# An attention block: the residual added by an accumulating transfer, more tiles for the first set, a later bias

## Chip, cores, metric

One core of one Trainium2 chip. The metric is the device time of one execution in microseconds (us), the median of several.

## The reference

Sixteen images of 512 channels x 1024 positions, in fp32: group norm, three projections, attention with four heads, an output projection, and the input added at the end.

```python
xn = ((xg - mu) * jax.lax.rsqrt(var + EPS)).reshape(b, c, h, w)
xn = xn * norm_gamma[:, None, None] + norm_beta[:, None, None]
qkv = jnp.einsum('oc,bchw->bohw', qkv_w, xn) + qkv_b[:, None, None]
...
attn = jax.nn.softmax(jnp.einsum('bhnd,bhmd->bhnm', q, k) * scale, axis=-1)
out = jnp.einsum('bhnm,bhmd->bhnd', attn, v)
...
out = jnp.einsum('oc,bchw->bohw', proj_w, out) + proj_b[:, None, None]
return x + out
```

## The kernel before

All products with weights are done by Strassen's scheme at two levels: seven outer products in four groups, seven inner products in each, so that TensorE multiplies less and VectorE adds more. While one head's attention runs (scores s, exponentials p, sums po), the other work is laid between its steps: under head 0 a q/k product, under head 1 the output projection of the image before and the norm of the next image, under head 2 the next q/k product, under head 3 the next v product. Line numbers in profiles shift a little between kernels; the names of the tiles do not.

The end of a projection, with its residual loaded ahead:

```python
        def prepare(which, r):                       # called some units ahead
            ...
            t = ys[which, r] = ypool.tile([P, HALF], F32, tag="y", ...)   # 4 buffers
            dma = nc.gpsimd.dma_start(t, x[b, ts(o, P), ts(half, HALF)])
            tc.add_manual_dep(dma.ins, last_eviction[b].ins.name, ...)

        def finish(which, r, a, c):
            ...
            nc.vector.scalar_tensor_tensor(t, a, projb_sb[:, o : o + 1], t, ALU.add, ALU.add)
            nc.vector.tensor_add(t, t, c)
            nc.gpsimd.dma_start(out[b, ts(o, P), ts(half, HALF)], t)
```

The norm's one instruction on GpSimd, and the last image's bias:

```python
        ve = gn.tile([P, k], F32, tag="ve", name="ve")
        self.last = nc.vector.tensor_scalar_add(ve, pv[:, :k], EPS)
        rstd = gn.tile([P, k], F32, tag="rstd", name="rstd")
        nc.gpsimd.tensor_tensor(rstd, ve, self.neghalf, ALU.pow)
        # cut: VectorE makes scale and shift of it, ScalarE then normalises the next image
    ...
    def last_bias():
        for c in range(NCC):
            nc.scalar.activation(late["y"][c], late["y"][c], AF.Identity, bias=projb_sb[:, c : c + 1])
```

## Time and profile before

| | before |
|---|---|
| time | 3199.4 us (five runs, 3198.9 to 3201.3) |
| span of the profiled run | 3198.0 us |
| TensorE, VectorE, ScalarE, GpSimd busy | 99, 82, 45, 17% |
| mean period of one image | 196.56 us |

The mean period is taken from GpSimd's timeline: the rstd instruction runs once per image, at 142.76 us for the second image and at 2894.55 for the last, so (2894.55 - 142.76) / 14. What lies ahead of the first of these is the start, what lies behind the last is the end.

### The profile page before, as it was taken

What the parts mean: (1) busy time and instruction counts of PE and PEld (TensorE: products, weight loads), DVE (VectorE), ACT (ScalarE), POOL (GpSimd) and SP (SyncE); (2) the same over time, 40 slices, a digit from 0 to 9 for tenths busy, and PEclk for the clock granted to TensorE, in tenths of its full rate; (3) what the DMA queues carried; (4) which work ended last, traced back from release to release, by engine and by line L of the source; (5) the groups of instructions that cost most, each with busy time, mean ns of one, the idle gap of its engine ahead of it and who ended that gap; (6) DMA issues with size and microseconds to landing.
All of it is one profiled execution on the core that took longest, in us unless ns stands there. A gap on an engine that the chain in (4) does not pass through costs nothing.

```text
span 3198.0 us, 34052 instructions
## 1 busy us (share of the span) xinstructions
PE 3161.4 (99%) x10474; PEld 2183.2 (68%) x10474; DVE 2633.2 (82%) x4625; ACT 1443.5 (45%) x2709; POOL 528.1 (17%) x922
## 2 busy tenths in 40 slices
PE   8999999999999999999999999999999999999999
PEld 6566676776766766677666676667676676766664
DVE  8878878788797888878788787987879978788784
ACT  2534435354353543535435454353534545344442
POOL 0011221112211112211122111222112221112100
PEclk9999999999999999999999999999999999999999
DMA  4565554545545455454554546555455564555531
GB/s 160 195 197 166 184 171 143 177 149 190 171 155 168 154 189 174 159 166 143 183 173 166 167 139 197 166 170 174 136 182 169 175 186 133 176 166 185 170 128 38
DMA packets 209387, 526.92 MB, mean 165 GB/s; under 512 B 32816, under 2 KB 65840, under 8 KB 209200
## 3 DMA queue, kind: packets, MB, share of 16 engines
q1 hardware_dynamic: 128992, 276.88, 28.5%
q0 software_dynamic: 66240, 212.39, 19.7%
q10 hardware_dynamic: 13968, 35.41, 3.5%
q8 instruction: 86, 1.41, 0.2%
q14 instruction: 101, 0.83, 0.1%
HBM read 389.56 MB, written 135.00 MB: 164 GB/s over the span
## 4 chain that ended last, share of the span: by engine, by line
PE 85%; DVE 6%; issue 3%; DMA 3%; ACT 2%; POOL 1%; SPq 0%; POOLq 0%; DVEq 0%
PE po L874 24%; PE s L778 23%; PE qk_x L553 12%; PE qk_y L553 8%; PE v_x L553 6%; PE v_y L553 4%; PE pp_x L553 4%; PE pp_y L553 3%; ACT x L85 1%; DMA y<-in_x 1%; DVE pp_r L620 1%; POOL rstd L67 1%; DVE pp_r L573 1%; DVE tot L792 1%; DVE o L884 1%
## 5 line engine op out<-in xcount | busy, mean ns | idle before, releaser
L874 PE MATMUL po<-p,v 128*128 128x512 f32 x2048 | 1049.2, 594 | 0.5 <-ACT o L881 0.5
L778 PE MATMUL s<-qk,qk 128*128 128x512 f32 x2048 | 1047.9, 593 | 1.3 <-ACT p L784 1.3
L784 ACT ACTIVATE p<-s 128x512 f32<-128x512 f32 x1024 | 610.8, 597 | 942.4 <-PE s L778 898.4
L874 PEld LDWEIGHTS po<-p,v 128*128 128x128 f32 x2048 | 602.9, 303 | 317.5 <-issue 211.4
L792 DVE TENSOR_TENSOR tot<-tot,p 128x1024 f32<-128x1024 f32 x385 | 469.0, 1218 | 160.0 <-ACT p L784 159.8
L778 PEld LDWEIGHTS s<-qk,qk 128*128 128x128 f32 x2048 | 387.6, 190 | 89.7 <-issue 28.5
L553 PEld LDWEIGHTS qk_x<-qk_t,w 128*128 128x128 f32 x1344 | 250.7, 190 | 176.9 <-issue 76.7
L553 PE MATMUL qk_x<-qk_t,w 128*128 128x256 f32 x1344 | 358.5, 383 | 4.5 <-ACT qk_u L453 3.0
L453 ACT COPY qk_u<-qk_x 128x512 f32<-128x512 f32 (+1 forms) x256 | 136.3, 532 | 232.0 <-PE qk_x L553 230.0
L717 POOL DMA_DIRECT2D vd<-vu x120 | 66.7, 557 | 906.9 <-DVE vu L709 903.0
L573 DVE TENSOR_TENSOR qk_r<-qk_y,qk_u 128x512 f32<-128x512 f32 (+1 forms) x256 | 158.0, 617 | 40.6 <-ACT qk_u L453 26.3
L553 PE MATMUL pp_x<-pp_t,w_proj 128*128 128x256 f32 x630 | 169.4, 385 | 5.9 <-ACT pp_u L453 5.7
L762 POOL DMA_DIRECT2D out_y<-y x120 | 66.2, 552 | 619.2 <-DVE y L761 589.0
L722 POOL DMA_DIRECT2D v<-vd x240 | 140.6, 593 | 164.3 <-DMA vd<-vu 58.7
L573 DVE TENSOR_TENSOR v_r<-v_y,v_u 128x512 f32<-128x512 f32 (+1 forms) x120 | 76.3, 636 | 110.6 <-ACT v_u L453 80.3
L553 PE MATMUL v_x<-v_t,w_v 128*128 128x256 f32 x630 | 166.6, 381 | 0.0
L527 POOL DMA_DIRECT2D kept_t<-qk_t x240 | 129.3, 541 | 225.9 <-DVE qk_t L523 158.4
L553 PEld LDWEIGHTS pp_x<-pp_t,w_proj 128*128 128x128 f32 x630 | 115.5, 190 | 73.0 <-issue 22.2
L553 PEld LDWEIGHTS v_x<-v_t,w_v 128*128 128x128 f32 x630 | 118.4, 190 | 55.3 <-issue 19.1
L553 PE MATMUL qk_y<-x,w 128*128 128x256 f32 x512 | 142.2, 379 | 0.0
L652 DVE SCALAR_TENSOR_TENSOR qk<-qk_r,qkb_sb,qk_r 128x512 f32<-128x512 f32 x192 | 137.6, 743 | 1.6
L453 ACT COPY v_u<-v_x 128x512 f32<-128x512 f32 (+1 forms) x124 | 66.3, 535 | 160.4 <-PE v_x L553 130.3
(204 smaller groups left out, 4483.2 us busy)
## 6 DMA issues: line engine op xcount, KB each, us to landing
kept_t<-qk_t POOLq DMA_DIRECT2D x180, 256.0 KB, 2.9
w<-kept SPq DMA_DIRECT2D x90, 512.0 KB, 4.1
v_t<-kept_t SPq DMA_DIRECT2D x180, 256.0 KB, 2.9
w<-kept SPq DMA_DIRECT2D x90, 384.0 KB, 3.5
rinv<-row ACTq DMA_DIRECT2D x63, 512.0 KB, 4.8
x<-in_x POOLq DMA_DIRECT2D x60, 512.0 KB, 4.4
vd<-vu POOLq DMA_DIRECT2D x120, 256.0 KB, 3.0
v<-vd POOLq DMA_DIRECT2D x240, 128.0 KB, 4.2
```

The costliest lines, as they stand in the source:

```text
L453: nc.scalar.copy(t[n][:, :width], t["x"][:, :width])
L527: nc.gpsimd.dma_start(t, to)
L553: nc.tensor.matmul(acc[:, ts(i, Q)], have["w"][t][:, i, slot, :], inner(i, bn), start=(first and i == 0), stop=True, skip_group_check=True,)
L573: nc.vector.tensor_add(dst, view(a), view(c))
L652: nc.vector.scalar_tensor_tensor(st[b, h][:, ts(half, HALF)], a, qkb_sb[:, i : i + 1], c, ALU.add, ALU.add)
L717: nc.gpsimd.dma_start(rows[which][ts(h, P), :], u)
L722: nc.gpsimd.dma_start(vs[b, pair][ts(q, BLK), half].rearrange("m h (k i) j -> m (h k) (i j)", k=n), rows[which].rearrange("(k m) (q e) -> ...
L762: nc.gpsimd.dma_start(out[b, ts(o, P), ts(half, HALF)], t)
L778: nc.tensor.matmul(sc, ks[b, h][:, ts(j, P)], qs[b, h][:, ts(half, HALF)], start=True, stop=True)
L784: exps[s] = nc.scalar.activation(ps[s][:, ts(half, HALF)], sc, AF.Exp, scale=SCALE)
L792: added[b, h, j] = nc.vector.tensor_add(tot[b, h][:, i], tot[b, h][:, i], ps[s][:, i])
L874: nc.tensor.matmul(po[b, h][:, i], v_block(b, h, j), ps[s][:, i], start=(j == 0), stop=(j == NB - 1),)
```

## The change

The intent is to take work off VectorE and to close gaps at both ends:

1. The residual is no longer loaded into y and added by VectorE. VectorE adds the two halves of the product and the bias, and a transfer that adds brings x into the finished tile; then the tile is stored. A load and 120 additions go.
2. In the first set, groups 1 and 3 take their sums of inputs in p buffers (homes "C"), and the weights of group 2 two idle tiles.
3. The last image's bias is placed behind an exponential on ScalarE.

```diff
+        own = first and (site, g) == (0, 2)
         w = [
-            wpool.tile([P, 2, m, P], F32, tag=f"w{t}", ...)
+            (lpool if own else wpool).tile([P, 2, m, P], F32, tag=("tt", "rinv")[t] if own else f"w{t}", ...)
 ...
+            if homes[g] == "C":
+                if k % 2 == 0:
+                    pairs[g] = ppool.tile([P, N], F32, tag="p", name=f"{name}_{g}_{m}")
+                t = pairs[g][:, ts(k % 2, HALF)]
 ...
-            "ABBB" if pair else "ABAB" if b > 0 else "BBBB",
+            "ABBB" if pair else "ABAB" if b > 0 else "BCBC",
 ...            # prepare() and its calls go
         def finish(which, r, a, c):
             ...
+            t = ypool.tile([P, HALF], F32, tag="y", ...)
             nc.vector.scalar_tensor_tensor(
-                t, a, projb_sb[:, o : o + 1], t, ALU.add, ALU.add
+                t, a, projb_sb[:, o : o + 1], c, ALU.add, ALU.add
             )
-            nc.vector.tensor_add(t, t, c)
+            nc.gpsimd.dma_start(t, x[b, ts(o, P), ts(half, HALF)], accum_op=ALU.add)
             nc.gpsimd.dma_start(out[b, ts(o, P), ts(half, HALF)], t)
 ...
     def last_bias():
+        with tc.issue_after(exps[max(exps)].ins):
             for c in range(NCC): ...
```

More of the change, by code (lines that the diff above doesn't have):

```diff
@@ L359, in group_weights @@
         n = len(group)
+        own = first and (site, g) == (0, 2)
         w = [
-            wpool.tile([P, 2, m, P], F32, tag=f"w{t}", name=f"w{t}_{site}_{g}")
+            (lpool if own else wpool).tile(
+                [P, 2, m, P], F32, tag=("tt", "rinv")[t] if own else f"w{t}",
+                name=f"w{t}_{site}_{g}",
+            )
             for t, m in enumerate(PARTS)
@@ L487, in strassen, with two_levels @@
         return [units[i] for i in ORDER]
-    def two_levels(name, site, b, blocks, finish, sums="make", homes="BBBB", prepare=None):
+    def two_levels(name, site, b, blocks, finish, sums="make", homes="BBBB"):
         R = {}
-        haves = [{} for _ in OUTER]
+        haves, pairs = [{} for _ in OUTER], {}
         def part(g, i, row=None):
@@ L504, in sum_tile @@
             tag = f"in_{m}" if homes[g] == "B" else f"ot{2 + k // 2}{k % 2}"
-            t = tpool.tile([P, HALF], F32, tag=tag, name=f"{name}_{g}_{m}")
+            if homes[g] == "C":
+                if k % 2 == 0:
+                    pairs[g] = ppool.tile([P, N], F32, tag="p", name=f"{name}_{g}_{m}")
+                t = pairs[g][:, ts(k % 2, HALF)]
+            else:
+                t = tpool.tile([P, HALF], F32, tag=tag, name=f"{name}_{g}_{m}")
             haves[g][m] = t.rearrange("p (i q) -> p i q", q=Q)
@@ L597, in group_units @@
                 unit(lambda: inner_sum("t3"), p2), unit(lambda: inner_sum("t4"), p6),
-                unit(lambda: load("t2"), lambda: ready(g), p5), unit(lambda: load("t1"), p7),
+                unit(lambda: load("t2"), p5), unit(lambda: load("t1"), p7),
                 unit(lambda: load("t3"), p4), unit(lambda: load("t4"), p3, end),
@@ L608, in first_sums @@
                         make_sum(g, m)
-        results = {1: ("c11",), 2: ("c22", "c21"), 3: ("c12",)}
-        def ready(g):
-            for which in results.get(g, ()) if prepare else ():
-                for r in range(2):
-                    prepare(which, r)
         pending = []
@@ L735, in proj_groups, with finish @@
     def proj_groups(b):
-        ys = {}
-        def place(which, r):
-            return 2 * (int(which[1]) - 1) + r, int(which[2]) - 1
-        def prepare(which, r):
-            o, half = place(which, r)
-            t = ys[which, r] = ypool.tile([P, HALF], F32, tag="y", name=f"y_{b}_{o}_{half}")
-            dma = nc.gpsimd.dma_start(t, x[b, ts(o, P), ts(half, HALF)])
-            tc.add_manual_dep(
-                dma.ins, last_eviction[b].ins.name,
-                mybir.DependencyInfo(
-                    mybir.DependencyClass.Sync, mybir.DependencyReason.DATA
-                ),
-                reason="residual",
-            )
-        def finish(which, r, a, c):
-            o, half = place(which, r)
-            t = ys.pop((which, r))
-            nc.vector.scalar_tensor_tensor(
-                t, a, projb_sb[:, o : o + 1], t, ALU.add, ALU.add
-            )
-            nc.vector.tensor_add(t, t, c)
+        def finish(which, r, a, c):
+            half, o = int(which[2]) - 1, 2 * (int(which[1]) - 1) + r
+            t = ypool.tile([P, HALF], F32, tag="y", name=f"y_{b}_{o}_{half}")
+            nc.vector.scalar_tensor_tensor(
+                t, a, projb_sb[:, o : o + 1], c, ALU.add, ALU.add
+            )
+            nc.gpsimd.dma_start(t, x[b, ts(o, P), ts(half, HALF)], accum_op=ALU.add)
             nc.gpsimd.dma_start(out[b, ts(o, P), ts(half, HALF)], t)
-        return two_levels(f"pp_{b}", "proj", b, lambda: ob[b], finish, prepare=prepare)
+        return two_levels(f"pp_{b}", "proj", b, lambda: ob[b], finish)
     ps, tot, po, rinv, last_eviction = {}, {}, {}, {}, {}
@@ L941, in last_bias @@
     def last_bias():
-        for c in range(NCC):
-            nc.scalar.activation(
-                late["y"][c], late["y"][c], AF.Identity, bias=projb_sb[:, c : c + 1]
-            )
+        with tc.issue_after(exps[max(exps)].ins):
+            for c in range(NCC):
+                nc.scalar.activation(
+                    late["y"][c], late["y"][c], AF.Identity, bias=projb_sb[:, c : c + 1]
+                )
     fine = []
```

## The prediction

> **What bounds the kernel now.** I read the page's busy rows first, then TensorE's clock and its waits, then the stretches where TensorE was not busy.
>
> ```profile
> PE 3161.4 (99%) x10474; PEld 2183.2 (68%) x10474; DVE 2633.2 (82%) x4625; ACT 1443.5 (45%) x2709; POOL 528.1 (17%) x922
> PEclk9999999999999999999999999999999999999999
> ```
>
> TensorE is busy in 3161.4 of 3198.0 us at full clock, and VectorE has 3198.0 - 2633.2 = 565 us free. Whatever the change does on VectorE can count only where TensorE stands waiting: 36.6 us of recorded idle in all. The view of waits, TensorE alone, the first 90 us and then 90 to 3150 us:
>
> ```profile
> PE pm L52 <- DVE mean L50: 10.6, 1, 10.6
> PE qk_x L553 <- DVE qk_t L523: 1.2, 1, 1.2
> PE qk_x L553 <- DVE w L390: 1.1, 1, 1.1
> ...
> PE pp_x L553 <- ACT pp_u L453: 5.7, 14, 0.4
> PE qk_y L553 <- DVE qk_t L523: 3.8, 4, 2.0
> PE qk_x L553 <- ACT qk_u L453: 2.4, 2, 1.5
> ```
>
> The columns are the total in us, the number of waits and the longest. The 10.6 us is the start, before the statistics are there. In the whole middle, 3060 us, VectorE makes TensorE wait 3.8 us in four waits, and no wait there names the residual tile y. The stretches view shows the two other holes. Its columns are PE, PEld, DVE, ACT, POOL busy time, with counts.
>
> ```profile
> 32.00:36.00 4.00, 4.00 (x20) 3.54 (x19) 1.92 (x6) 0.59 (x1) 0.00 (x0) 1.00 0.92 325
> 36.00:40.00 4.00, 4.00 (x19) 3.36 (x19) 1.26 (x3) 1.17 (x2) 0.00 (x0) 1.00 0.24 72
> 40.00:44.00 4.00, 4.00 (x20) 3.53 (x19) 2.06 (x5) 0.93 (x2) 0.00 (x0) 1.00 0.25 66
> ...
> 56.00:60.00 4.00, 2.96 (x13) 1.79 (x11) 4.00 (x8) 1.50 (x3) 0.00 (x0) 1.00 0.25 84
> 60.00:64.00 4.00, 2.69 (x10) 1.74 (x10) 3.91 (x7) 0.64 (x2) 0.00 (x0) 1.00 0.11 33
> 64.00:68.00 4.00, 2.25 (x8) 1.28 (x9) 3.94 (x11) 0.57 (x2) 0.00 (x0) 1.00 0.32 113
> 68.00:72.00 4.00, 3.56 (x11) 1.83 (x11) 3.79 (x8) 1.14 (x3) 0.00 (x0) 1.00 0.22 63
> ```
>
> From 32 to 44 us VectorE has 12 - (1.92 + 1.26 + 2.06) = 6.8 us free while TensorE is full; from 56 to 72 us VectorE is full (15.6 of 16 us) and TensorE lacks 16 - (2.96 + 2.69 + 2.25 + 3.56) = 4.5 us. This is the first set: VectorE is the bound for some 16 us there, because it could not start earlier. The second hole is late, in the chain that ended last:
>
> ```profile
> 3007.51 5.78 DMA y<-in_x
> ...
> 3023.44 7.30 DMA y<-in_x
> ...
> 3056.59 5.56 DMA y<-in_x
> ```
>
> These loads are not the residuals of the projections but the last image's, which a ScalarE bias (line 943) takes up at once. The waits of this stretch have "ACT y L943 <- DMA y<-in_x: 9.6, 4, 2.8". ScalarE runs in order, so its copies out of PSUM stand behind. In the stretches of 5 us TensorE lacks 1.52 us (3010 to 3015), 0.84 (3030 to 3035) and 0.48 (3060 to 3065): 2.8 us.
>
> **What the Trainium skill says.** (1) "Perfetto Trace Analysis", section Per-engine timelines, Tensor Engine: matmul ends are estimated. The trace agrees: eight 128x256 matmuls in a row take 1.73 us in the chain, 0.216 us each, while their mean row says 379 to 385 ns. So I also count: one image has 4 x 98 matmuls of 128x256 and 256 of 128x512 (0.430 us each), 84.7 + 110.1 = 194.8 us of work, and its period is 1122.04 - 925.65 = 196.4 us (starts of the rstd instruction in the chain). Only 1.6 us per image is open to any change. (2) "VectorE: DVE Perf Modes": fp32 tensor_tensor takes (N+151)/0.96 ns, 691 ns for 512. The trace has 682 ns for line 761, about the same. (3) "DMA: Bandwidth & Descriptors", Rules for kernel authors: an accumulating DMA is issued from GpSimd, reads its destination and writes it later, and a dependent access has to wait for its semaphore. So the store of y must wait on GpSimd until the addition has landed. No accumulating transfer is in the trace before. (4) The same page, Anatomy of one DMA: 2.0 us + bytes / 436e3, so 2.6 us for 256 KB. The trace has 4.0 us for the residual's load and 2.9 for the store; I use those.
>
> **The change part by part.**
>
> *Residual.* Removed: 120 additions at line 761 x 682 ns = 81.8 us of VectorE, and 120 loads of 256 KB. Line 758 stays one scalar_tensor_tensor of the same shape, 120 x 745 ns, now adding the two products. Added: 120 accumulating transfers, issued at 0.54 us each like line 745, so GpSimd's issue time stays equal. VectorE falls to about 2551 us. Nearly all of that lies under TensorE's work: per image 81.8 / 15 = 5.5 us in a stretch of 50 us where VectorE has 16% free. At the end of each projection VectorE is dense, and the norm's small operations come between; finishing those 0.7 to 1.4 us sooner may start the normalisation sooner, but the wait seen there is on ScalarE's pp_u copy (0.4 us per image), behind normalisations on ScalarE that stay as long as they are. I give it -1 us over 15 images.
>
> *More tiles for the first set.* Groups 1 and 3 of the first product take their sums from the p buffers in place of the tiles that group 0 and 2 hold, and the weights of group 2 take two idle tiles. The release that ends the waits is a read by TensorE: the waits of the SP queue have
>
> ```profile
> SPq L375 <- PE qk_y L553: 32.2, 10, 9.8
> ```
>
> and the timeline has the sums for group 1 first at 42.54 us after an idle of VectorE. Eight sums at about 0.37 us back to back are 3.0 us, two s3 blocks and four weight sums at 0.41 us are 2.5 us: 5.5 us of VectorE work can move into the 6.8 us that are free. With VectorE that much earlier from 44 us on, the 4.5 us hole should shrink by the same, but not wholly: p has three buffers, four such pair tiles want them, and the finishes still come at TensorE's pace. I take 4.0 us of 4.5.
>
> *Last bias.* It is put behind an exponential that is already issued, so the loads have landed when ScalarE comes to it. Saved: the 2.8 us. Cost: four 128x1024 activations of 1.15 us now stand among exponentials that are spaced 1.72 us apart at 0.60 us each; a score tile can come about 0.1 us late each time. I take 2.5 us net.
>
> Sum: -1.0 - 4.0 - 2.5 = -7.5 us on 3200.6, that is 3193.
>
> **The rivals.**
>
> *The store waits on GpSimd, and VectorE behind it.* The y pool has 4 buffers. Before, a tile was free one store (2.9 us) after its last addition; now it goes through the addition (about 4.0 us, estimated from the load) and then the store: some 8 us with issues. Six finishes fall within 1127 to 1139 us of the example image, so the fifth and sixth take tiles of the first and second of that burst. If GpSimd issues strictly add, wait, store, a pair takes some 5 us and VectorE would wait about 2 to 5 us at line 758; and the copies kept_t, which stand next on GpSimd (1140 us), would go out late and hold tiles that the next sums need. For it: the queue is in order, and already now
>
> ```profile
> POOL y L745 <- DMA out_y<-y: 85.3, 44, 4.3
> POOL out_y L762 <- DVE y L761: 589.0, 84, 61.5
> ```
>
> so it does wait on stores. Against it: the same 85.3 us cost TensorE nothing, several additions can be issued before the first store, and VectorE has slack. If it were so, TensorE would lose up to 1 to 3 us per image: +15 to +45 us, 3208 to 3238. I give it 12%.
>
> *The 82 us of VectorE count.* If VectorE set the end, 3200.6 - 81.8 = 3119 us would come. Against it: 3.8 us of waits in the middle. Even all 1.6 us of each of 15 images would be only -24 us, 3169 with the ends. I give 5% to more than -16 us.
>
> *The transfer is hidden and the ends do not gain.* If the first hole is bound by something else (the weights' own loads, or three p buffers), the 4.0 us stay away: 3197 us. 20%.
>
> **Range and chances.** The middle of these is 3193. The ends give -3 to -8 us; the projections give -6 to +10 us. So 3184 to 3205 should hold 8 times in 10, the upper arm longer because of the store's wait. Faster by over 2% would need 3137 us: 64 us, more than all recorded idle, 1%. Slower by over 2% would need 3265 us, over 4 us lost in each image: 2%.
>
> **What would show it.** Right: TensorE's busy time about equal and the span some 7 us shorter; VectorE busy near 2551 us; no 4.5 us lack between 56 and 72 us, and the first scores earlier than 68.0 us; no ScalarE wait on the last loads near 3010 us; the period per image still about 196.4 us. Wrong: waits of line 758 on a DMA, a kept copy waiting behind a store on GpSimd, an accumulating transfer that takes well over 4 us to land, a period that grows by more than 0.5 us, or TensorE waiting on qk_t at the start of each next image. A period under 195.9 us would show that VectorE did matter.

## More of the kernel before

The page's line on the chain that ended last, before:

```profile
PE 85%; DVE 6%; issue 3%; DMA 3%; ACT 2%; POOL 1%; SPq 0%; POOLq 0%; DVEq 0%
```

It is TensorE's for most of the way.

## The result, and the profile after

| | before | after |
|---|---|---|
| time, five runs each | 3199.4 us | 3229.2 us (3226.0 to 3233.2) |
| ratio | | 1.0091, 95% interval 1.0077 to 1.0105 |
| rstd of the second image at | 142.76 us | 136.48 us |
| mean period | 196.56 us | 198.94 us |
| last rstd to the end | 303.5 us | 302.6 us |

A ratio is the mean time of one kernel's fast runs over that of the other's of the same rounds, so not quite the ratio of the medians. The changed kernel is slower by 0.9%. Start and end gain 6.3 and 0.9 us, and the 14 periods lose 14 x 2.38 = 33.3 us; together +26.1, the difference of the two spans (3224.1 - 3198.0).

First the two halves that went as foreseen. The stretches of 56 to 72 us after the change (columns as in the prediction):

```profile
56.00:60.00 4.00, 4.00 (x20) 3.16 (x19) 4.00 (x6) 1.68 (x4) 0.00 (x0) 1.00 0.10 28
60.00:64.00 4.00, 3.54 (x17) 2.69 (x15) 4.00 (x8) 1.33 (x3) 0.73 (x1) 1.00 0.10 24
64.00:68.00 4.00, 3.33 (x13) 2.20 (x12) 3.75 (x9) 1.46 (x3) 0.00 (x0) 1.00 0.73 275
68.00:72.00 4.00, 4.00 (x15) 2.54 (x14) 4.00 (x12) 1.33 (x3) 0.00 (x0) 1.00 0.47 162
```

TensorE lacks 1.1 us there instead of 4.5. The last image begins some 27 us later now (its rstd at 2921.6 us instead of 2894.5), and its late loads go out from 3034.8 to 3081.0 us; TensorE is full in every stretch of 5 us from 3010 to 3110 us.

Now the loss. The page's busy row and its chain line after the change:

```profile
PE 3161.0 (98%) x10474; PEld 2185.4 (68%) x10474; DVE 2563.3 (80%) x4505; ACT 1440.8 (45%) x2709; POOL 565.7 (18%) x922
...
PE 66%; issue 19%; DVE 6%; DMA 6%; POOL 2%; ACT 0%; SPq 0%; POOLq 0%; ACTq 0%; DVEq 0%
```

VectorE is busy 70 us less (120 additions of 682 ns would be 81.8, but the records of neighbours overlap: two in a row take 1.28 us), TensorE the same, and yet the chain runs through issue and transfers much more. The waits of TensorE, VectorE and GpSimd after the change (total us, times, longest):

```profile
PE pp_x L563 <- ACT pp_p L458: 20.8, 14, 1.6
PE qk_y L563 <- DVE qk_r L583: 19.5, 13, 1.8
...
DVE y L743 <- DMA out_y<-y: 47.8, 20, 4.7
DVE sc L69 <- POOL rstd L67: 26.4, 15, 2.4
...
POOL out_y L748 <- DMA y<-in_x: 250.0, 100, 4.7
```

Read from below: the store stands on GpSimd 250 us in all for the addition to land. Behind it stands rstd, so VectorE waits for rstd (26.4 us, 14.6 before). And y tiles come free late, so VectorE waits for them (47.8 us; before, it waited 5.7 us for y loads and never for a store). TensorE has two waits of 1.5 us in the mean (1.6 and 1.8 at most) in nearly each image that it did not have. GpSimd's timeline in one image, before:

```profile
1119.40 0.54 POOL L745 DMA_DIRECT2D y<-in_x  x1 [3.15 <-DMA out_y<-y]
1122.04 1.88 POOL L67 TENSOR_TENSOR rstd<-ve,neghalf 128x4 f32<-128x4 f32 x1 [2.10 <-DVE ve L65]
1129.61 1.15 POOL L762 DMA_DIRECT2D out_y<-y  x2 [5.69 <-DVE y L761]
```

and after, in the same part of an image:

```profile
1120.76 1.78 POOL L747 DMA_DIRECT2D y<-in_x  x2 [30.09 <-DVE y L743]
1125.05 0.58 POOL L748 DMA_DIRECT2D out_y<-y  x1 [2.50 <-DMA y<-in_x]
1128.88 0.57 POOL L748 DMA_DIRECT2D out_y<-y  x1 [3.26 <-DVE pp_r L583]
1129.47 1.05 POOL L67 TENSOR_TENSOR rstd<-ve,neghalf 128x4 f32<-128x4 f32 x1
1133.63 2.85 POOL L747 DMA_DIRECT2D y<-in_x  x3 [3.12 <-DVE y L743]
```

Before, rstd went out when ve was ready. After, it comes straight behind the second store (no idle is noted before it), though ve had been ready since 1128.0 us; the store ahead of it is noted as waiting for a VectorE instruction, but the store reads only y, and what it needs is the second addition. What follows on the other engines after the change, all engines by time:

```profile
1130.55 0.16 DVE L69 TENSOR_TENSOR sc<-rstd,gamma_sb 128x4 f32<-128x4 f32 x1 [1.74 <-POOL rstd L67]
...
1132.37 0.81 ACT L85 ACTIVATE x<-x,sh,sc 128x512 f32<-128x512 f32 x1 [1.92 <-DVE sh L78]
...
1133.09 0.35 ACT L458 COPY pp_p<-pp_x 128x256 f32<-128x256 f32 x1
...
1133.49 0.70 PE L563 MATMUL pp_x<-pp_t,w_proj 128*128 128x256 f32 x2 [1.52 <-ACT pp_p L458]
...
1145.20 1.61 DVE L743 SCALAR_TENSOR_TENSOR y<-pp_r,projb_sb,pp_r 128x512 f32<-128x512 f32 x2 [3.40 <-DMA out_y<-y]
```

The scale comes late, ScalarE stands in order before the first normalisation, the copy pp_p out of PSUM stands behind that, and TensorE loses 1.52 us. Some 12 us later VectorE stands 3.40 us for a y tile, with the next image's sums and evictions behind it. From there it runs without a gap, and at 1161.38 us TensorE has stood 1.80 us for its qk_r: the wait of qk_y.

The rows of transfers show why all this is longer than I had reckoned. From before (KB each, median us from issue to landing), then from after:

```profile
y<-in_x POOLq DMA_DIRECT2D x120, 256.0 KB, 4.0
```

```profile
y<-in_x POOLq DMA_DIRECT2D x120, 256.0 KB, 6.5
```

The adding transfer took 6.5 us to land, not 4.0, and its issue on GpSimd 0.95 us in the median, not 0.54.

**Theory.** The adding transfer is slow, and the store must wait for it in GpSimd's order: (A) rstd comes late, (B) y tiles come free late. **Rivals:** the extra tiles of the first set or a changed order cost throughout; the adding transfers cost by themselves (load on the transfer engines, issue time); it is the waiting in the queue alone, whatever the transfer.

### The profile page after: what moved, and what is told of

Read it like the earlier page. It is cut to its first block, busy times and chain, and to the rows that moved or that the text cites.

```text
span 3224.1 us, 33936 instructions
## 1 busy us (share of the span) xinstructions
PE 3161.0 (98%) x10474; PEld 2185.4 (68%) x10474; DVE 2563.3 (80%) x4505; ACT 1440.8 (45%) x2709; POOL 565.7 (18%) x922
## 3 DMA queue, kind: packets, MB, share of 16 engines
q0 software_dynamic: 73920, 212.39, 22.2%
HBM read 389.56 MB, written 135.00 MB: 163 GB/s over the span
## 4 chain that ended last, share of the span: by engine, by line
PE 66%; issue 19%; DVE 6%; DMA 6%; POOL 2%; ACT 0%; SPq 0%; POOLq 0%; ACTq 0%; DVEq 0%
PE s L764 18%; PE po L860 18%; PE qk_x L563 10%; PE qk_y L563 7%; PE v_x L563 6%; PE v_y L563 4%; DMA y<-in_x 3%; DVE qk_t L533 2%; DMA out_y<-y 2%; DVE xt L280 1%; DVE qk_r L583 1%; POOL y L747 1%; DVE part L789 1%; POOL rstd L67 0%; DVE tt L787 0%
## 5 line engine op out<-in xcount | busy, mean ns | idle before, releaser
L747 POOL DMA_DIRECT2D y<-in_x x120 | 109.4, 1038 | 537.2 <-DVE y L743 525.0
L563 PE MATMUL pp_x<-pp_t,w_proj 128*128 128x256 f32 x630 | 169.3, 385 | 20.8 <-ACT pp_p L458 20.8
L537 POOL DMA_DIRECT2D kept_t<-qk_t x240 | 143.4, 600 | 107.9 <-DVE qk_t L533 92.5
L655 DVE SCALAR_TENSOR_TENSOR qk<-qk_r,qkb_sb,qk_r 128x512 f32<-128x512 f32 x192 | 137.7, 744 | 1.6
L563 PE MATMUL qk_y<-qk_t,w 128*128 128x256 f32 x448 | 119.1, 382 | 19.5 <-DVE qk_r L583 19.5
```

What stands on the lines that cost most here:

```text
L537: nc.gpsimd.dma_start(t, to)
L563: nc.tensor.matmul(acc[:, ts(i, Q)], have["w"][t][:, i, slot, :], inner(i, bn), start=(first and i == 0), stop=True, skip_group_check=True,)
L655: nc.vector.scalar_tensor_tensor(st[b, h][:, ts(half, HALF)], a, qkb_sb[:, i : i + 1], c, ALU.add, ALU.add)
L747: nc.gpsimd.dma_start(t, x[b, ts(o, P), ts(half, HALF)], accum_op=ALU.add)
```

## The experiments

### e1: the residual as before, the rest of the change kept

```diff
# after.py with prepare(), ready() and finish() of before.py
```

> The changed kernel with the residual put back as before (a load, then an addition on VectorE); the tiles of the first set and the late bias stay. Theory (the new residual alone costs, through the store that waits for the addition): the period per image is back at 196.4 us and the ends gain what the trace of after shows (6.3 us before the second image's rstd, about 1 us at the end), so 3200 - 7 = 3193 us. Rival (the first set's extra tiles or the other order cost through the whole run): stays above 3215 us.

Measured: 3190.6 us, ratio 0.9970 (0.9954 to 0.9987) to before. rstd of the second image at 138.1 us, period 196.49, end 299.8 us. The loss is the residual's; the rest of the change gains. The gain at the start is 4.6 us where the changed kernel shows 6.3, so up to 2 us of the latter may come with the other order.

### e2: the new residual alone on the kernel before

> The kernel before with the new residual alone. Theory (the new residual costs 2.4 us in each of 15 images, the rest of the change gains 8 us as the run with the old residual showed): 3199 + 36 = 3230 to 3238 us, period 198.9 us. Rival (the extra tiles of the first set shift the order, and so cause part of the loss): under 3222 us.

Measured: 3233.7 us, ratio 1.0102 (1.0085 to 1.0119), period 198.99 us. As the theory has it; the rival of the extra tiles falls.

### e11 and e12: the tiles alone, the bias alone

> The kernel before with the extra tiles for the first set alone. Theory: the hole of TensorE at 56 to 72 us shrinks, second image's rstd 4.6 us earlier (138.1 instead of 142.8 as in the run with the old residual), nothing else: 3194 to 3196 us. Rival (the tiles gain nothing by the end): 3199.

Measured: 3193.6 us, ratio 0.9982 (0.9963 to 1.0001); rstd of the second image at 137.7 us, 5.1 us earlier; TensorE busy 14.86 of 16 us from 56 to 72 us, where the run of e12 without the tiles has 11.46.

> The kernel before with the late bias behind an exponential alone. Theory: TensorE's three holes from 3010 to 3065 us (2.8 us in sum) go, and nothing else moves: 3196 to 3197 us. Rival (given back among the exponentials): 3199.

Measured: 3196.8 us, ratio 0.9985 (0.9969 to 1.0002). The three stretches of 5 us of the former holes are full and the end is 3.9 us shorter (299.6 us). In this one profiled run, though, the second image's rstd came 1.0 us later than before (143.8 us) and the period was 196.75, so its span (3197.8 us) is no shorter; TensorE, VectorE and GpSimd have the same instructions in the same order as before, and still the periods of the two profiles differ by 0.2 us. Both intervals just reach 1, so by time alone each is unclear; the profiles show that each closes its hole, and e1, which has both, is clearly faster.

### e5b: only the two stores that stand before rstd leave GpSimd

```diff
-            nc.gpsimd.dma_start(out[b, ts(o, P), ts(half, HALF)], t)
+            (nc.sync if which == "c11" else nc.gpsimd).dma_start(out[b, ts(o, P), ts(half, HALF)], t)
```

TensorE, VectorE and ScalarE have the same instructions in the same order as in the changed kernel.

> Only the two stores per image that stand before rstd on GpSimd (block c11) go out from SP; the other six stay on GpSimd. Order on the other engines is the same. Theory in two halves: (A) rstd behind a store costs about 1.1 us per image on TensorE (pp_x waits 1.5 us for ScalarE's pp_p instead of 0.4), (B) the late y tiles cost 1.8 us (qk_y waits for qk_r). This takes A away alone: pp_x's wait falls to about 0.4 us, qk_r's stays, 3226 - 15 = 3211 us. If A and B overlap, less; if only B counts, 3226.

Measured: 3203.3 us, ratio 1.0008 (0.9991 to 1.0025), period 197.16 us. TensorE's waits in this run:

```profile
PE qk_y L563 <- DVE qk_r L583: 16.3, 16, 2.0
...
PE pp_x L563 <- ACT pp_p L458: 2.8, 14, 0.2
```

The wait for pp_p is gone, that for qk_r is there. VectorE's wait for rstd fell from 26.4 to 6.8 us. So A is shown. The edit as a whole gives 198.94 - 197.16 = 1.8 us per image, more than the 1.1 that I had put. Not all of it need be A: the pp_p wait alone fell by (20.8 - 2.8) / 14 = 1.3 us, and with two of eight stores gone GpSimd also stood less before the others (182.2 us instead of 250.0) and VectorE less for y tiles (34.8 instead of 47.8).

### e5: all eight stores leave GpSimd, for SP

```diff
-            nc.gpsimd.dma_start(out[b, ts(o, P), ts(half, HALF)], t)
+            nc.sync.dma_start(out[b, ts(o, P), ts(half, HALF)], t)
```

> The changed kernel, but the store of y goes out from the SP queue instead of GpSimd's, so GpSimd never waits for an addition to land. Order on TensorE, VectorE and ScalarE is the same, instruction for instruction. Theory (GpSimd's in-order queue stands behind the store's wait: rstd late, further additions late, y tiles held): most of the 2.4 us per image returns, 3193 to 3203 us. Rival (the accumulating transfer's own length, 6.5 us to landing, or its load on the DMA engines): y tiles are still held, 3220 us or more. SP could itself hold up weight loads: then waits of qk_x or pp_x on DMA w appear.

Measured: 3218.7 us, ratio 1.0058 (1.0041 to 1.0075), period 198.47 us: a miss, close to the rival's 3220. A is gone (the pp_p wait is 2.8 us in all), but VectorE waits 55.8 us for y tiles, more than in the changed kernel, and TensorE 28.0 us for qk_r. SP is in order too; its own waits, before it issues, in this run:

```profile
SPq L371 <- PE qk_y L563: 1029.2, 195, 10.8
...
SPq L748 <- DMA y<-in_x: 324.4, 120, 8.8
```

The weights' loads stand there up to 10.8 us for TensorE to release a buffer, and the stores stand for their additions up to 8.8 us. The six stores of a burst share that queue with the weights, which fits that the tiles are not free sooner. Here a queue that waits for something else was no better home. The run does not show how much of the 6.5 us counts.

### e6: the same queue and waits, with a plain transfer

```diff
-            nc.gpsimd.dma_start(t, x[b, ts(o, P), ts(half, HALF)], accum_op=ALU.add)
+            nc.gpsimd.dma_start(t, x[b, ts(o, P), ts(half, HALF)])
```

The result lacks the projection. Every engine has the same instructions in the same order as in the changed kernel.

> Wrong on purpose: the transfer overwrites y with x in place of adding, so the result lacks the projection; every instruction and wait is the same. Theory (waits in the queue, whatever kind of transfer stands in them): the landing falls from 6.5 to about 4 us, the waits shrink with it but the structure stays: 3200 to 3215 us. Rival (the cost is only that additions are slow): near 3193 us. Second rival (the kind doesn't matter at all): 3226 us.

Measured: 3180.4 us, ratio 0.9940 (0.9923 to 0.9956), period 195.95 us. This is a miss for my own theory: I had expected the structure of waits to cost something with any transfer. The issue of the transfer on GpSimd (ns: least, median, most), in the changed kernel, then in this one, whose landing follows:

```profile
L747 POOL DMA_DIRECT2D y<-in_x x120: 856/952/1553, 323.3 to 3139.6; - x120
```

```profile
L747 POOL DMA_DIRECT2D y<-in_x x120: 538/543/604, 323.0 to 3094.1; - x120
...
y<-in_x POOLq DMA_DIRECT2D x120, 256.0 KB, 4.5
```

GpSimd still stands 206.9 us for these transfers before its stores (250.0 in the changed kernel), yet VectorE waits only 7.4 us for y tiles, and TensorE's two waits are 2.8 and 0.8 us in all. So the wait in the queue costs nothing as long as it ends before someone needs what is behind it: with 4.5 us to landing it does, with 6.5 us and 0.4 us more of issue it does not. That is the cause, and it is worth 198.94 - 195.95 = 3.0 us per image. Landing and issue were not told apart.

And e6 is 0.54 us per image faster than e1, some 8 us in the run. I took this as what the VectorE time that the change saves is worth. The traces also show another difference: the rstd instruction itself takes 1.88 us in the median in e1 (and in the kernel before), 1.04 us in e6. In e1 an addition of 128x1024 stands beside it on VectorE in 13 of 16 images, and rstd ends 0.90 us after that addition each time; in e6 another VectorE instruction, of 128x512, stands there. VectorE's wait for rstd is 14.5 us in e1 and 6.8 in e6. So part of the 0.54 us can be what stands beside rstd, which no run tested alone.

### e9 and e9b: adding into the output in HBM

If the addition is the last transfer, no store waits for it, and a tile is held for one transfer only. The output must hold x before.

```diff
+    def prefill(b):
+        prefilled[b] = nc.sync.dma_start(out[b], x[b])      # under head 0 of the next image
-            nc.gpsimd.dma_start(t, x[b, ts(o, P), ts(half, HALF)], accum_op=ALU.add)
-            nc.gpsimd.dma_start(out[b, ts(o, P), ts(half, HALF)], t)
+            dma = nc.gpsimd.dma_start(out[b, ts(o, P), ts(half, HALF)], t, accum_op=ALU.add)
+            tc.add_manual_dep(dma.ins, prefilled[b].ins.name, ...)
```

> The changed kernel, but x is copied to the output in HBM ahead of time (SP queue, one 2 MB copy per image, 50 us or so early), and the finished tile goes out by one transfer that adds to the output in HBM. No store waits for an addition, a y tile is free after one transfer. Theory (two slow transfers one behind the other, in order on GpSimd and holding a y tile, are the cost; VectorE's saved addition is worth 0.6 us per image as the plain-load run showed): the period falls from 198.9 to about 196.0 us, 3178 to 3186 us. Rival (an adding transfer costs by itself, 0.95 us of GpSimd issue each and load on the DMA engines): the period stays above 197 us, 3198 us or more.

Measured: right result, 3284.5 us, ratio 1.0262 (1.0245 to 1.0279). Nothing made a copy wait, so the scheduler put all 15 copies of 2 MB between 18 and 418 us. TensorE's longest waits:

```profile
PE qk_x L563 <- DMA w<-kept: 34.0, 1, 34.0
PE po L873 <- DMA v<-vd: 25.0, 2, 14.9
```

The second image's rstd came at 198.3 us in place of 136.5; late in the run the period was 196.1 us. In the next run each copy waits for its image's last eviction (ScalarE's copy of the last attention sum out of PSUM):

```diff
+        tc.add_manual_dep(prefilled[b].ins, last_eviction[b].ins.name, ...)
```

> The addition into the output in HBM again, but each image's copy of x to the output waits for that image's last eviction, so the copies come one per image and not all in the first 418 us. Theory: the 85 us lost in the first run of this form came from the bunched copies (TensorE waited 34 us on w<-kept and 25 us on v<-vd), while its later period was 196.1 us already; so now 3198 - 6 (first set) - 1 (last bias) - 14 x 0.45 = about 3183 us, period 196.1 us, faster than both kernels. Rival (the 4 MB more of HBM traffic per image costs somewhere else in each image): 3195 us or more.

Measured: right result, 3181.9 us (3181.5 to 3184.3), ratio 0.9948 (0.9934 to 0.9962), period 196.11 us. This is faster than both kernels. Its adding transfers still take as long to land:

```profile
out_y<-y POOLq DMA_DIRECT2D x120, 256.0 KB, 6.5
```

Their issue takes 0.91 us in the median. So neither costs by itself where nothing waits behind; VectorE waits 0.5 us for y tiles, and TensorE's wait for pp_p is 2.8 us in all. The profile counts 166.46 MB written to HBM instead of 135.00, 2.1 MB more per image, and no more read; this extra traffic does not show in the period. The rival of the adding transfers' own cost falls. The order on the engines is not the changed kernel's here, so e6, which keeps it, and e9b have to be read together.

### e13: the saved VectorE time given back

```diff
+            nc.vector.tensor_add(t, a, c)                    # overwritten by the next line
             nc.vector.scalar_tensor_tensor(t, a, projb_sb[:, o : o + 1], c, ALU.add, ALU.add)
```

> The same, with one dummy addition of 128x512 on VectorE put ahead of each final one (120 x 0.68 us = 82 us of VectorE, the time that the change was to save; the result stays right). Theory (VectorE's saved time is worth about 0.5 us per image, as the period of the plain-load run, 195.95 against 196.49 with the old residual, suggests): 8 us slower than without it, period 196.6 us. Rival (that difference came from where the transfers and rstd stand, not from VectorE): within 2 us of it.

Measured: right result, 3198.6 us, ratio 0.9998 (0.9984 to 1.0012), period 197.17 us, VectorE busy 2639.6 us. It is 16.7 us slower than e9b, twice what I expected. TensorE's waits in it:

```profile
PE pp_y L563 <- DVE pp_t L533: 6.2, 14, 0.4
PE pp_x L563 <- DVE pp_t L533: 5.7, 14, 0.4
```

So the dummy additions (VectorE busy 69.8 us more than in e9b, 4.7 us per image) go with 1.06 us per image. The order on the engines changed as well (a scheduler places the instructions), so the number is not VectorE's alone: rstd takes 2.01 us in the median here and 1.04 in e9b, 0.97 us more, again with an addition of 128x1024 beside it. What VectorE's time alone is worth is not shown.

## Why the prediction was wrong

- **Ends.** Predicted -4.0 us for the tiles; e1 and e11 show 4.6 and 5.1 us earlier. Predicted -2.5 us for the bias; e12 shows 3.9 us at the end of the span, and e1 against e11 2.5 us (299.8 and 302.3). These steps held.
- **The step that failed** is the residual's term, "-1 us over 15 images". Measured, from e1 to the changed kernel, it is +35.3 us of span (3224.1 - 3188.8). Under it lie two sizes: "the addition (about 4.0 us, estimated from the load)" was 6.5 us, and "GpSimd's issue time stays equal" was 0.54 to 0.95 us. e6 shows that these sizes decide: with 4.5 us and 0.54 us the same order of instructions ran in 3180 us, better than predicted.
- **Right rival, wrong weight.** The rival of the store's wait was named with 3208 to 3238 us, and 3229 us lies in it, but it got 12%. Its counter-argument, that GpSimd already stood 85.3 us for stores at no cost, looked at the length of a wait and not at what stands behind it. Before, loads that nobody needed at once stood there. After, rstd did, and the prediction did not name that path at all: it is 1.3 us per image by TensorE's own wait, up to 1.8 by e5b's period, of the 3.0 us between the changed kernel and e6; that the y tiles and what follows from them are the rest is by subtraction.
- **VectorE's worth.** I took TensorE's recorded waits on VectorE, 3.8 us in the middle, as the bound of what less VectorE work could give. e6 against e1 gives 7.6 us over 14 periods (0.54 us each), e13 against e9b 1.06 us each in the other direction. So the bound failed. By what path is open: in both pairs rstd on GpSimd takes longer, by 0.84 and 0.97 us, in the run with more work on VectorE, and a wait for GpSimd or ScalarE does not carry VectorE's name.
- **Markers.** The prediction's own signs of error came: VectorE waiting for a transfer before the y instruction, a landing well over 4 us, a period up by more than 0.5 us. The kept copies too take longer to land (5.5 us instead of 2.9), but as long in e6, so they are not the loss.
- **Open.** Whether the longer landing or the longer issue matters more, how much of e5b's gain is rstd's alone, and how much of e6's gain over e1 is VectorE's time, rstd's own length or the other order of instructions.

## What to carry to other kernels

A transfer that is cheap in engine time may still be slow to land; when a second transfer must wait for it on an in-order queue, look for what stands behind that wait and when it is needed, not for the wait's length. If an accumulating transfer is wanted, make it the last one, into a destination filled ahead of time, and tie the filling to its time, since without a dependency it can all move to the front. And the waits that name one engine did not bound what relief of it was worth.

## What the Trainium skill lacked or had wrong

- "DMA: Bandwidth & Descriptors" gives no time for an accumulating transfer. Here 256 KB took 6.5 us to landing in the median (4.5 us plain, same place and waits, e6), 0.91 to 0.95 us of GpSimd per issue against 0.54, and 64 packets more each ((73920 - 66240) / 120 on GpSimd's queue). Into HBM it was 6.5 us as well (e9b).
- Its section Anatomy of one DMA gives 2.0 us + bytes / 436e3, by estimate 2.6 us for 256 KB; the kernel before, with other transfers under way, shows 2.9 us for the store and 4.0 us for the load in the median.
- Its Rules for kernel authors say rightly that a dependent access waits for the accumulating transfer's semaphore. They give no size for what stands behind that wait on the issuing engine: here rstd, 1.3 us per image by TensorE's wait and up to 1.8 by the period (e5b).
